# A mixture-of-experts stage on one core: TensorE branches on each expert's token count

## The chip, the cores and the metric

The kernel runs on one core of one Trainium2 chip. The metric is the device time of one execution in microseconds, given as the median of several runs. The profile is of one execution, taken by the hardware profiler; its span runs from the first to the last instruction and is a little shorter than the device time of the same execution.

The engines are TensorE (PE; its weight loads are listed apart, as PEld), VectorE (DVE), ScalarE (ACT), GpSimd (POOL) and SyncE (SP). Each works through its own queue of instructions in order. A matmul loads a 128x128 stationary operand and streams the columns of the other operand through it. A float32 matmul stands in the trace as two passes, each a weight load and a MATMUL record; a transpose by the identity is one pass.

## What is computed

One layer: graph attention over 3327 nodes, then a mixture of 16 experts of which each token takes two. The second half is what the change touches:

```python
logits = jnp.einsum('bsd,de->bse', x, gate_w) + gate_b
probs = jax.nn.softmax(logits, axis=-1)
top_probs, top_idx = jax.lax.top_k(probs, 2)
top_probs = top_probs / jnp.sum(top_probs, axis=-1, keepdims=True)
dispatch = jnp.sum(jax.nn.one_hot(top_idx, n_experts) * top_probs[..., None], axis=-2)
h1 = jnp.einsum('bsd,edh->bseh', x, w1)
h2 = jnp.einsum('bsd,edh->bseh', x, w2)
hidden = jax.nn.silu(h1) * h2
expert_out = jnp.einsum('bseh,eho->bseo', hidden, w3)
return jnp.einsum('bseo,bse->bso', expert_out, dispatch)
```

A token has 256 features, the hidden size is 512, all in float32. The inputs are fixed, and so is the routing. Evaluated on them, the reference sends these numbers of tokens to the experts 0 to 15:

```
351 473 404 471 511 387 336 393 505 414 372 404 387 375 473 398     (sum 6654 = 2 x 3327)
```

## The kernel before, in words

The first part (the graph attention and the routing, lines 153 to 447) ends with a table: `index[:, e, t]` holds, for expert `e` and row tile `t` of 128 places, the token that stands in each place, or a number out of bounds where the place is empty. An expert has 512 places (`CAP`), four row tiles (`CT`). `count` (L433) is the number of tokens of each expert. From it `chunks` and `more` say whether an expert has more than 512; for these inputs none has, and the second loop behind L533 is jumped over.

The second part works through the 16 experts, one after the other:

- `begin(e)` calls `fetch` (L465): four indirect DMAs on POOL (L468) gather the expert's rows, with their gate weights, into one of three buffers `xe0`, `xe1`, `xe2`, used in turn. Two short DVE instructions (L472 `hit`, L474 `weight`) then take the gate weight out of the rows; `hit` waits for all four DMAs.
- `turned` (L477): eight transposes on TensorE (L482) into PSUM, two ACT copies (L483), give `xte`, the transposed tokens, 2 blocks of 128 features by 512 places.
- `up` (L486): for each of four blocks `j` of 128 hidden units, four matmuls (L494; two blocks of features, for `w1` and for `w2`) give `p1` and `p2`, each 128x512 in PSUM. ACT makes `s = silu(p1)` (L497), DVE makes `hid[:, j] = s * p2` (L498). `p1` and `p2` have two PSUM buffers each.
- `down` (L501): for each of four row tiles `t`, four matmuls (L506; one for each `j`) give `py`, 128x256, in one of two PSUM buffers. DVE scales it by the gate weight into `y` (L509), and POOL adds it to the rows of `out` by an indirect DMA (L510); places that are out of bounds are not written.
- `load_expert` (L144): three DMAs on SP bring the next expert's weights.

The program gives a scheduler the instructions; it decides the order in each engine's queue and puts the semaphore waits. In the built program before the change the order on TensorE is, for every expert, up(e), the transposes for e+1, down(e), without any other work between them. On DVE `hit` for a later expert stands among the instructions of down, and on POOL the four gathers for a later expert stand next to the four additions to `out`.

All 512 places are multiplied, empty or not: the empty rows of `xe` hold zeros or old, finite data, and their results are not written.

## Time and profile before

| | |
|---|---|
| median of 3 runs | 642.27 us (642.19 to 642.32) |
| the profiled execution | 642.2 us; its span 640.4 us |
| first transpose of the expert stage (L482) | 279.0 us after the start of the span |
| last matmul of the expert stage (L506) | ends at 631.0 us |
| mean granted TensorE clock | 0.959 |

A line of a group gives the source line, the engine and the operation, the tile written and the tiles read, the shape and the count; behind the bar the busy time in us and the mean duration of one in ns; behind the second bar the time that the engine stood idle just before such instructions, and what ended most of it. MATMUL records overlap, so their mean is longer than their distance. An engine name with a q behind it (PEldq, SPq) means an instruction that the engine's sequencer does by itself, as a branch, a register load or a wait.

### The profile page before, as it was taken

To read this page: it belongs to the slowest core of one execution; us is meant where nothing else is said; L and a number is where in the kernel's file an instruction comes from. 1 tells how busy PE (TensorE), PEld (TensorE's weight loads), DVE (VectorE), ACT (ScalarE), POOL (GpSimd) and SP (SyncE) were. 2 spreads that over 40 slices of the span, in tenths; PEclk is the share of its full clock that TensorE was granted. 3 is DMA by queue.
4 is the path that set the end of the run, shared out by engine and by line. 5 is a ranking of instruction groups with operands and counts; after the bars stand their busy time and mean duration, and the time that the engine had idled before them with its cause. 6 is when DMAs were issued, how large, how long until landed. Compare 5 with 4: busy or idle time off the path is not lost. (4 is left out here: it accounts for less than half of the span.)

```text
span 640.4 us, 8294 instructions
## 1 busy us (share of the span) xinstructions
PE 584.6 (91%) x2906; PEld 430.7 (67%) x2907; DVE 271.4 (42%) x896; ACT 165.7 (26%) x472; POOL 209.4 (33%) x181
## 2 busy tenths in 40 slices
PE   1999999999999994459999999999999999999994
PEld 0778999999999993324566556656665666566653
DVE  4853576869687777722221222122212222222221
ACT  2666435151524244111111211121112111111110
POOL 2442100101010102055563356335533653333123
PEclk9999999899999996559999999999999999999998
DMA  7975488596858531124463445344534553444022
GB/s 251 389 217 200 140 272 271 165 328 225 296 178 317 188 95 64 67 54 122 90 148 94 102 112 153 104 94 109 142 101 98 118 145 100 85 97 117 8 30 28
DMA packets 65006, 94.71 MB, mean 148 GB/s; under 512 B 6331, under 2 KB 35135, under 8 KB 64960
## 3 DMA queue, kind: packets, MB, share of 16 engines
q1 hardware_dynamic: 51552, 79.75, 37.4%
q0 software_dynamic: 12288, 13.76, 12.8%
q10 hardware_dynamic: 1120, 0.61, 0.3%
q8 instruction: 24, 0.39, 0.2%
q14 instruction: 22, 0.18, 0.1%
HBM read 82.01 MB, written 15.26 MB: 152 GB/s over the span
## 5 line engine op out<-in xcount | busy, mean ns | idle before, releaser
L414 PE MATMUL pa<-hi,mk 128*128 128x258 f32 x676 | 169.1, 289 | 0.0
L415 PE MATMUL pa<-lo,mk 128*128 128x256 f32 x676 | 167.4, 287 | 1.5 <-DVE lo L215 1.5
L415 PEld LDWEIGHTS pa<-lo,mk 128*128 128x128 f32 x676 | 128.6, 190 | 1.9 <-DVE lo L215 1.7
L414 PEld LDWEIGHTS pa<-hi,mk 128*128 128x128 f32 x676 | 129.1, 191 | 0.2
L510 POOL DMA_INDIRECT out<-y,index x64 | 100.7, 1574 | 72.0 <-DVE y L509 55.3
L494 PE MATMUL p<-xte,w1e 128*128 128x512 f32 x256 | 122.2, 600 | 0.5 <-ACT xte L483 0.5
L494 PE MATMUL p<-xte,w2e 128*128 128x512 f32 x256 | 120.9, 595 | 1.5 <-DVE hid L498 1.5
L506 PE MATMUL py<-w3e,hid 128*128 128x256 f32 x512 | 113.2, 379 | 0.0
L498 DVE TENSOR_TENSOR hid<-s,p 128x512 f32<-128x512 f32 x64 | 43.9, 687 | 161.5 <-PE p L494 121.5
L468 POOL DMA_INDIRECT xe<-normed,index x64 | 65.5, 1023 | 132.4 <-PE pt L482 104.1
L497 ACT ACTIVATE s<-p 128x512 f32<-128x512 f32 x64 | 38.2, 597 | 258.5 <-PE p L494 258.5
L506 PEld LDWEIGHTS py<-w3e,hid 128*128 128x128 f32 x512 | 96.2, 190 | 12.8 <-issue 0.5
L494 PEld LDWEIGHTS p<-xte,w2e 128*128 128x128 f32 x256 | 48.8, 191 | 63.9 <-issue 60.8
L494 PEld LDWEIGHTS p<-xte,w1e 128*128 128x128 f32 x256 | 49.1, 192 | 55.8 <-issue 53.6
L375 DVE TENSOR_SCALAR mk<-sg 128x2048 fp32r<-128x2048 f32 (+2 forms) x49 | 52.5, 1072 | 30.5 <-PE pa L415 27.8
L509 DVE TENSOR_SCALAR y<-py,weight 128x256 f32<-128x256 f32 x64 | 30.1, 483 | 58.6 <-PE py L506 58.6
L172 POOL TENSOR_TENSOR rs_x<-rs_x,neg_half 128x4 f32<-128x4 f32 (+1 forms) x14 | 16.2, 1154 | 78.5 <-DVE rs_x L171 61.9
L172 POOL TENSOR_TENSOR rs_hp<-rs_hp,neg_half 128x4 f32<-128x4 f32 (+1 forms) x7 | 6.8, 969 | 107.2 <-DVE pay L333 49.4
L213 PE MATMUL ph<-w_sb,xnt 128*128 128x260 f32 x104 | 28.2, 414 | 1.5 <-DVE er L216 1.2
L266 ACT ACTIVATE hp<-csum,c 128x64 f32<-128x64 f32 x104 | 25.7, 334 | 13.8 <-DVE c L262 13.8
L177 ACT ACTIVATE pay<-x,rs_x 128x256 f32<-128x256 f32 x26 | 13.7, 591 | 59.8 <-DVE rs_x L173 59.8
L483 ACT COPY xte<-pt 128x512 f32<-128x512 f32 x32 | 17.2, 589 | 38.1 <-PE pt L482 38.1
(123 smaller groups left out, 442.8 us busy)
## 6 DMA issues: line engine op xcount, KB each, us to landing
sg<-in_adj_t SPq DMA_DIRECT2D x36, 1024.0 KB, 6.4
w1e<-in_ffn_w SPq DMA_DIRECT2D x16, 512.0 KB, 3.4
w2e<-in_ffn_w SPq DMA_DIRECT2D x16, 512.0 KB, 4.2
w3e<-in_ffn_w SPq DMA_DIRECT2D x16, 512.0 KB, 4.4
sg<-in_adj_t SPq DMA_DIRECT2D x12, 512.0 KB, 3.7
normed<-pay SPq DMA_DIRECT2D x6, 520.0 KB, 3.3
x<-in_x SPq DMA_DIRECT2D x6, 512.0 KB, 9.3
out<-x SPq DMA_DIRECT2D x6, 512.0 KB, 4.4
```

The costliest lines, as they stand in the source:

```text
L213: nc.tensor.matmul(ph, xnt[:, k, :], w_sb[:, k, :], start=(k == 0), stop=(k == KC - 1))
L266: nc.scalar.mul(hp[:, t, h * DH:(h + 1) * DH], csum[:, h * DH:(h + 1) * DH], c[:, 1, t, h:h + 1])
L375: nc.vector.tensor_scalar(mk[:, :M, :T * P], sg[:, :M, :T * P], 0.0, None, op0=ALU.is_gt)
L414: nc.tensor.matmul(pa[t], lhs, HI[mg][:, m, :], start=first, stop=False)
L415: nc.tensor.matmul(pa[t][:, :D], lhs, LO[mg][:, m, :], start=False, stop=last)
L468: nc.gpsimd.indirect_dma_start(out=xe[:, t, :], out_offset=None, in_=normed, in_offset=at_rows(idx, t), bounds_check=NP - 1, oob_is_err=False)
L494: nc.tensor.matmul(p, wt[:, k, j * P:(j + 1) * P], xt[:, k, :], start=(k == 0), stop=(k == KC - 1))
L497: nc.scalar.activation(s, p1, AF.Silu)
L498: nc.vector.tensor_mul(hid[:, j, :], s, p2)
L506: nc.tensor.matmul(py, hid[:, j, t * P:(t + 1) * P], w[2][:, j, :], start=(j == 0), stop=(j == JC - 1))
L509: nc.vector.tensor_scalar(y, py, weight[:, t:t + 1], None, op0=ALU.mult)
L510: i = nc.gpsimd.indirect_dma_start(out=out, out_offset=at_rows(idx, t), in_=y, in_offset=None, bounds_check=NP - 1, oob_is_err=False, comp ...
```

## The change

TensorE no longer multiplies all 512 places. From `count` DVE makes a table `width`: for each expert a number 0 to 4, which says the smallest of 384, 416, 448, 480 and 512 that holds its count, and a number 0 or 1, which says whether the count is over 384. TensorE loads these numbers into registers (32 loads in all). In `up`, for every `j`, it takes one of five arms, each with the same four matmuls at another number of columns. In `down`, at the last row tile, it takes one of two arms: the four matmuls, or none. The other engines do the same work as before, on the full 512 columns. So that they find finite numbers there, the PSUM tiles are no longer taken from a pool in turn, but are six fixed tiles, which DVE sets to zero once.

```diff
+WIDTHS = [384, 416, 448, 480, 512]
...
+    width = const.tile([P, 2, NE], I32, name="width")
...
         nc.vector.tensor_copy(count, pl[:, :NE])
 
+        bounds = tiny.tile([P, len(WIDTHS) - 1], F32, name="bounds", bufs=1)
+        over = tiny.tile([P, NE, len(WIDTHS) - 1], F32, name="over", bufs=1)
+        widthf = tiny.tile([P, 2, NE], F32, name="widthf", bufs=1)
+        nc.gpsimd.iota(bounds, pattern=[[WIDTHS[1] - WIDTHS[0], len(WIDTHS) - 1]], base=WIDTHS[0], channel_multiplier=0,
+                       allow_small_or_imprecise_dtypes=True)
+        nc.vector.tensor_tensor(over, count[:, :, None].to_broadcast([P, NE, len(WIDTHS) - 1]),
+                                bounds[:, None, :].to_broadcast([P, NE, len(WIDTHS) - 1]), op=ALU.is_gt)
+        nc.vector.tensor_reduce(widthf[:, 0], over, AX.X, ALU.add)
+        nc.vector.tensor_scalar(widthf[:, 1], count, float(CAP - P), None, op0=ALU.is_gt)
+        nc.vector.tensor_copy(width, widthf)
...
-        ps_h = ffn.enter_context(tc.tile_pool(name="ps_h", bufs=2, space=bass.MemoryType.PSUM))
-        ps_y = ffn.enter_context(tc.tile_pool(name="ps_y", bufs=2, space=bass.MemoryType.PSUM))
+        sums = ffn.enter_context(tc.tile_pool(name="sums", bufs=1, space=bass.MemoryType.PSUM))
...
-        def up(w, xt):
+
+        P1, P2, PY = ([sums.tile([P, size], F32, name=f"{name}{i}") for i in range(2)]
+                      for name, size in (("p1", CAP), ("p2", CAP), ("py", D)))
+        for p in P1 + P2 + PY:
+            nc.vector.memset(p, 0.0)
+
+        def arms(choice, n):
+
+            if choice is None:
+                yield n - 1
+            else:
+                yield from tc.Switch({mybir.EngineType.PE: choice}, n)
+
+        def up(w, xt, choice=None):
             t1, t2, _ = w
             hid = hidden.tile([P, JC, CAP], F32, name="hid")
             for j in range(JC):
-                p1 = ps_h.tile([P, CAP], F32, name="p1")
-                p2 = ps_h.tile([P, CAP], F32, name="p2")
-                for p, wt in ((p1, t1), (p2, t2)):
-                    for k in range(KC):
-                        nc.tensor.matmul(p, wt[:, k, j * P:(j + 1) * P], xt[:, k, :],
-                                         start=(k == 0), stop=(k == KC - 1))
+                p1, p2 = P1[j % 2], P2[j % 2]
+                for case in arms(choice, len(WIDTHS)):
+                    cols = WIDTHS[case]
+                    for p, wt in ((p1, t1), (p2, t2)):
+                        for k in range(KC):
+                            nc.tensor.matmul(p[:, :cols], wt[:, k, j * P:(j + 1) * P], xt[:, k, :cols],
+                                             start=(k == 0), stop=(k == KC - 1))
                 s = gates.tile([P, CAP], F32, name="s")
...
-        def down(w, hid, idx, weight):
+        def down(w, hid, idx, weight, choice=None):
             done = []
             for t in range(CT):
-                py = ps_y.tile([P, D], F32, name="py")
-                for j in range(JC):
-                    nc.tensor.matmul(py, hid[:, j, t * P:(t + 1) * P], w[2][:, j, :],
-                                     start=(j == 0), stop=(j == JC - 1))
+                py = PY[t % 2]
+                for case in arms(choice if t == CT - 1 else None, 2):
+                    for j in range(JC if case else 0):
+                        nc.tensor.matmul(py, hid[:, j, t * P:(t + 1) * P], w[2][:, j, :],
+                                         start=(j == 0), stop=(j == JC - 1))
...
+        def choice(i, e, top):
+            return nc.tensor.value_load(width[0:1, i, e:e + 1], min_val=0, max_val=top)
+
...
         for e in range(NE):
-            hid = up(WE[e], xt)
+            hid = up(WE[e], xt, choice(0, e, len(WIDTHS) - 1))
...
-            down(WE[e], hid, *ready.pop(e)[1:])
+            down(WE[e], hid, *ready.pop(e)[1:], choice(1, e, 1))
```

The scheduler orders a program of many blocks otherwise than one long block. This is TensorE's queue from the middle of the program, written down from the built program (`py(t,j)` is one matmul of row tile `t`; "waits" gives what a semaphore wait is for; e is an even expert, the pair repeats):

```
transposes for e+2 (last 4) around py(0,0) py(0,1) py(1,0) py(1,1) of e
switch up e+1, j=0
py(0,2) py(1,2) of e
switch up e+1, j=1
py(0,3) py(1,3) of e;  2 transposes for e+3;  py(2,0) of e: waits y of tile 0
switch tile 3 of e: waits y of tile 1
py(2,1) py(2,2) py(2,3) of e;  6 transposes for e+3
switch up e+1, j=2
py(0,0) py(1,0) of e+1
switch up e+1, j=3
py(0,1) py(1,1) of e+1
switch up e+2, j=0: its p2 waits hid of e+1, j=2
py(0,2) of e+1
switch up e+2, j=1: its p2 waits hid of e+1, j=3
py(0,3) py(1,2) py(1,3) of e+1;  py(2,0) of e+1: waits y of tile 0;  py(2,1)
switch tile 3 of e+1: waits y of tile 1
py(2,2) py(2,3) of e+1
switch up e+2, j=2;  4 transposes for e+4;  switch up e+2, j=3
```

And these are the queues of POOL and DVE over the same stretch:

```
POOL: gather 0 for the buffer that the transposes for e+2 left; add y2, y3 of e-1; gathers 1 2 3;
      add y0, y1 of e; gather 0 for the next buffer; add y2, y3 of e; gathers 1 2 3; add y0, y1 of e+1; ...
DVE:  hid of e j=2, j=3;  hit (waits the four gathers);  y0 y1 of e;  y2 y3 of e;  hid of e+1 j=0, j=1;
      hit (waits the next four gathers);  hid of e+1 j=2, j=3;  y0 y1 of e+1; ...
```

At the start the order is another one: before the first `up` stand five register loads, the transposes of expert 0 and two transposes of expert 1; then up of expert 0 for j=0 and j=1; then the other six transposes of expert 1, all eight of expert 2, and nine register loads among and behind them; then j=2 and j=3 of expert 0 with four matmuls of its down, and eight register loads; then up of expert 1.

## The prediction

> **What bounds the kernel now.** I read the page's engine line first, then the table of stretches from the middle of the expert stage, then the costliest groups, then the timelines of the queues that the change reorders.

> ```profile
> span 640.4 us, 8294 instructions
> PE 584.6 (91%) x2906; PEld 430.7 (67%) x2907; DVE 271.4 (42%) x896; ACT 165.7 (26%) x472; POOL 209.4 (33%) x181
> ...
> 320.00:400.00 80.00, 80.00 (x275) 49.34 (x274) 18.44 (x39) 12.65 (x22) 40.87 (x32) 1.00 0.50 121
> ...
> L494 PE MATMUL p<-xte,w2e 128*128 128x512 f32 x256 | 120.9, 595 | 1.5 <-DVE hid L498 1.5
> ...
> L506 PE MATMUL py<-w3e,hid 128*128 128x256 f32 x512 | 113.2, 379 | 0.0
> ```

> From 320 to 400 us TensorE is busy 80.00 of 80 us at clock 1.00, and its idle time before `py` is 0.0: the array is the whole cost there. An expert takes (631.0 - 279.0) / 16 = 22 us on average. The timeline gives 0.429 us from one 512-column pass to the next, 0.838 ns a column, and half that for a 256-column pass. Per expert: 32 passes x 0.429 + 32 x 0.2147 + 8 transposes x 0.11 = 13.7 + 6.9 + 0.9 = 21.5 us.

> ```profile
> L510 POOL DMA_INDIRECT out<-y,index x64 | 100.7, 1574 | 72.0 <-DVE y L509 55.3
> ...
> 326.45 1.00 POOL L468 DMA_INDIRECT xe<-normed,index  x1 [0.30 <-issue]
> 327.75 0.99 POOL L468 DMA_INDIRECT xe<-normed,index  x1 [0.30 <-issue]
> 329.05 1.62 POOL L510 DMA_INDIRECT out<-y,index  x1 [0.31 <-issue]
> 330.98 1.57 POOL L510 DMA_INDIRECT out<-y,index  x1 [0.31 <-DVE y L509]
> ...
> DVE hit L472 <- DMA xe<-normed,index: 57.2, 16, 7.0
> ...
> 330.17 0.17 DVE L472 SCALAR_TENSOR_TENSOR hit<-xe 128x8 f32<-128x8 f32 x1 [2.42 <-DMA xe<-normed,index]
> ```

> POOL needs 1.30 us from one gather to the next and 1.87 for an addition. `hit` waits 57.2 us in all for gathers and starts 2.2 to 4.2 us (median 2.84) after the last gather's start. Before the change this is hidden: the work behind it on DVE is not yet due.

> **Gain.** By the counts the widths are 384, 480, 416, 480, 512, 416, 384, 416, 512, 416, 384, 416, 416, 384, 480, 416: 6912 columns where there were 8192. 1280 x 32 passes x 0.838 ns = 34.3 us. Four experts (0, 6, 10, 13) have at most 384 and skip a tile of 8 passes, 1.72 us: 6.9. Sum 41.2 us, if TensorE stays fed.

> **DVE before the stage.** The six zeroings stand on DVE, with one more small instruction (`full`, 0.27 us) than before, ahead of `index`, on which the first gather waits. The 128x64 memset of before took 0.112 us, the 128x4 one 0.062: 0.83 ns an element gives 0.49 for 512 columns and 0.27 for 256, 2.5 in all; PSUM operations of those shapes took 0.687 and 0.483, together 3.7; lower end 2.1, if each starts 0.07 before the one ahead of it ends, as DVE's neighbours do here. I take 2.7 with `full`, bare on the path to the first gather. Three small ones of the width table stand there too, in the places of three of the `chunks` table, two of which move behind `index`.

> **Start.** Two transposes of expert 1 now stand before the first `up`, so it waits for a gather issued at 282.69: + 2.84 + 0.2 + a switch (0.83, below) = 286.5, where it was 283.38.

> ```profile
> 282.69 1.00 POOL L468 DMA_INDIRECT xe<-normed,index  x1 [0.30 <-issue]
> ...
> 287.81 0.21 PEld L494 LDWEIGHTS p<-xte,w2e 128*128 128x128 f32 x1 [0.52 <-issue]
> ...
> 290.50 1.00 POOL L468 DMA_INDIRECT xe<-normed,index  x1 [0.30 <-issue]
> ...
> L532 PEldq TENSOR_LOAD <-more x1: 493/493/493, 628.2 to 628.2; - x1
> L532 SPq FUSED_REGOPS  x1: 191/191/191, 275.9 to 275.9; - x1
> ...
> L533 PEldq COMPARE_BRANCH  x1: 373/373/373, 628.8 to 628.8; - x1
> L533 SPq COMPARE_BRANCH  x1: 50/50/50, 589.3 to 589.3; - x1
> ```

> Weight loads were 0.85 us apart until 287.8 and 0.43 after: for its first 4.4 us the array ran at half speed. So j=0 and j=1 (16 x 0.322 = 5.15, and 2.25 for the half speed) end at 293.9. Expert 2's transposes wait for the gather of 290.50, landed at 293.3; among and behind them stand register loads of 0.493 + 0.191 + 0.028 (assertion) = 0.71 us each: with seven of them and a switch j=2 starts at 299.2, the array idle for 3.8; eight more loads idle it for about 2. Expert 1 then begins at 308.1, where it was 308.8. But eight `py` matmuls are still owed (3.4), eight transposes already done (-0.9), and expert 0's whole saving of 5.15 is spent: -0.7 + 3.4 - 0.9 + 5.15 = 7.0. The idle may bring the half speed back: 0 to 2.3, I take 1.2. Start: 8.2. The other nine loads run ahead under queued matmuls; uncovered they would be 6.4.

> **The new DVE waits.** In the new order `hit` for a later expert stands on in-order DVE ahead of work that TensorE needs.
> - A: ahead of y0, y1 of experts 4, 6, 8 and 10. From the transposes that free the buffer: POOL 0.30, gather 1.30, two additions 3.74, two gathers 2.60 to the last one's start, 2.84 landing, `hit` 0.17, y0 0.48: 11.4. TensorE has 8 `py` and 3 transposes (3.77) and two up blocks of 8 x 416 x 0.838 ns = 2.79: 9.35. Wait 2.1, with handoffs 2.3; four: 9.1.
> - B: ahead of `hid` j=2 of experts 2, 3, 5, 7 and 9, for which the p2 of two switches later waits. From y0: four additions 7.48, three gathers 3.90, 2.84, `hit` 0.17, `hid` 0.69, handoffs 0.7: 15.8. TensorE has 4.6 of fixed work, 1.72 if the tile is kept, two up blocks of that expert and half of one of the next. For expert 5: 15.8 - 4.6 - 1.72 - 5.58 - 1.29 = 2.6; the five: 2.3, 1.4, 2.6, 3.9, 2.6 = 12.8.

> Together 22, and by the spread of the landing 18 to 27. Jumps on POOL between blocks lengthen both chains: 23 at about 0.1 (between SP's 0.05 and its 0.19 to the next instruction): 2.3.

> **The switches.** The trace has one compare and branch on TensorE's sequencer, 0.373 us; on SP it took 0.050. With register work a switch has 0.83 before its first matmul, 1.3 to the end. Where the sequencer is ahead of the array, as in the middle of `up` (it was 2.5 to 5.4 us ahead in the trace), that is hidden. It is not hidden at the switch of tile 3, behind the wait for y0, with 0.43 of `py` queued: 0.8 for each of eight even experts with y0's own handoff, 0.35 for each of eight odd, 0.5 for each of four empty arms: 11. Bounds: 4 by SP's row, 20 if each of 80 also shows 0.12 more.

> [...]

> **Sum**: -41.2 + 2.7 + 8.2 + 22 + 2.3 + 11 = +5. The profiled execution took 642.2 (span 640.4 and 1.8 around it), the median is 642.27: **647 us**. Its own range, adding the terms' bounds in part: 638 to 660.

> **Rivals.**
> - *Code misses (slower, far).* Each taken jump may find its target not yet loaded. The page counts instruction packets, 24 of 16 KB:

> ```profile
> q8 instruction: 24, 0.39, 0.2%
> ```

>   After the change TensorE's program has some 470 instructions an expert, arms not taken included: 29 packets of 256. The only jump of before, at 628.8, was followed by nothing for 2.3 us; that gap also holds the array's drain, so 2.3 is an upper end. At half of it, 29 x 1.15 = 33: 680 us; at 80 misses of 1.0 it passes 720. For it: that gap. Against: jumps that stay within a packet, and the sequencer's lead. It decides when a miss is longer than the lead. [...]
> - *The waits A and B do not come (faster).* If the last gather landed some 2.5 us earlier than my chains have it, both vanish: 647 - 22 - 2.3 = 623; if half of them, 635. For it: `hit` is never late in the trace of before, and POOL is busy for 33% only. Against: the spacing of 1.30 and 1.87 is the same in every expert, and a shorter `up` makes the cover shorter, not the chain.
> - *The narrower pass is no shorter.* If a pass were bound by its weight load, 34.3 us of the gain would be gone: 681. Against: weight loads took 0.19 us, a pass of 384 takes 0.322.

> **How the numbers follow.** Likeliest case 0.55, misses 0.18, no or half waits 0.23, no shorter pass 0.04. From 633 (half of the waits, some exposure less) to 680 (misses at half price) leaves out about 2 in 10. A measurement of this kernel tells a change of 0.2%, 1.3 us, from none: within it (641.0 to 643.6) I put 0.07, nearly all from the likeliest case; faster gets the second rival and a tenth of the likeliest, 0.29; slower the rest, 0.64.

> **What would show it.** The first gather 2.7 us later than 275.9. `up` passes 0.32 to 0.43 us apart by width; 0.43 everywhere speaks for the third rival. TensorE idle before `py` for y, and before `p2` for `hid`, about 2 us each at nine places, with `hit` just ahead of them on DVE; none of it: the second. An idle array around j=2 of expert 0 with register loads on PEldq. Branch records on PEldq of 0.3 to 0.5 us; gaps of over 1 us behind them with no wait, and many more than 24 instruction packets: the first. I am wrong if TensorE's idle time lies at places where no wait and no switch stands, or if the up blocks are paced by ACT or DVE, which still work on 512 columns: per j 0.60 and 0.69 us against 2.57, so far from it.

## The result and the profile after

The changed kernel takes 1075.85 us (median of 4 runs, 1072.97 to 1081.21) beside 642.23 of the kernel before on the same chip: 1.677 times as long, 95% interval 1.670 to 1.684. The prediction said 647, between 633 and 680. The sign was right; the size was off by 429 us. Ratios here and below leave out executions over 1.5% above the fastest of their kernel, which are four of the ten of `blocks`, its profiled one (650.4 us) among them.

The page of the profile after, the lines that answer to those shown of before (the rows of tenths are the span in 40 slices; PEclk is the granted TensorE clock):

```profile
span 1075.5 us, 9119 instructions
PE 705.3 (66%) x2874; PEld 474.7 (44%) x2875; DVE 269.6 (25%) x906; ACT 166.2 (15%) x472; POOL 210.0 (20%) x182
PE   3999999994455356566656664776666465675554
PEclk9999999996587667878888787786778768766777
q8 instruction: 297, 4.87, 2.5%
L521 PE MATMUL p<-xte,w1e 128*128 128x416 f32 (+3 forms) x256 | 182.5, 861 | 209.5 <-issue 207.2
L534 PE MATMUL py<-w3e,hid 128*128 128x256 f32 x480 | 141.9, 435 | 95.6 <-issue 95.0
```

Three things are to be seen. TensorE, which before stood idle 2.0 us before `up` and 0.0 before `down`, stands idle 207 us before the passes of `up` and 95 us before those of `down`, and what ended these waits is "issue": no DMA and no other engine that the profile shows, which leaves its own sequencer. The granted clock is at 0.5 to 0.8 from the tenth slice on, where the array is busy for 3 to 7 tenths of a slice. And the instruction queue (q8) moved 297 packets of 16 KB where it moved 24.

The view of the line under which the jumps are recorded (count, then least, median and greatest duration in ns, first and last start), for TensorE's sequencer and for DVE's:

```profile
L617 PEldq COMPARE_BRANCH  x160: 295/4497/5877, 289.1 to 1060.6; - x160
L617 PEldq FUSED_REGOPS  x80: 32/32/41, 289.0 to 1057.0; - x80
L617 DVEq COMPARE_BRANCH  x80: 41/41/53, 285.7 to 1057.2; - x80
```

There are two jumps to a switch, into the arm and out of it, 160 in all, with a median of 4.5 us. The 80 jumps of DVE, which only lead on to the next block, took 0.04 each. In a window from the middle, 600 to 660 us, the sequencer is hardly ever out of a jump, 14 of 4.5 us in 60 us:

```profile
L617 PEldq COMPARE_BRANCH  x14: 1507/4489/5209, 596.4 to 656.2; - x14
```

and the array beside it (start, duration, engine, line, operation, count of records, in brackets the idle time ahead):

```profile
614.00 2.92 PE L521 MATMUL p<-xte,w1e 128*128 128x384 f32 x4 [2.28 <-issue]
616.70 2.77 PE L521 MATMUL p<-xte,w2e 128*128 128x384 f32 x4
619.39 0.70 PE L495 MATMUL pt<-ident,xe 128*128 128x128 f32 x4
622.50 2.48 PE L521 MATMUL p<-xte,w1e 128*128 128x384 f32 x4 [2.40 <-issue]
...
655.83 2.93 PE L534 MATMUL py<-w3e,hid 128*128 128x256 f32 x6 [6.54 <-issue]
```

Adding up the 160 records gives 666 us; from the start of the first to the end of the last are 774 us. Which packets began to arrive during each jump, and where the jump led, I counted from the trace's records (which arm is taken follows from the counts):

| jump | number | packets begun in it | median us |
|---|---|---|---|
| into arm 384, the first behind the dispatch | 16 | 1 (two jumps: 0) | 2.9 (0.3) |
| into a later arm of `up` | 48 | 2 (four jumps: 1) | 4.5 |
| out of arm 512, the last before the common end | 8 | 1 | 3.1 |
| out of an earlier arm of `up` | 56 | 2 (one jump: 1) | 4.7 |
| tile 3, into and out of the arm with matmuls | 24 | 1 | 3.4 |
| tile 3, into the empty arm, and out of it | 4 + 4 | 0 (one jump: 1), then 2 | 1.7, then 4.7 |

A jump during which no packet began took 0.3 to 2.0 us (5 of them), with one 3.3 in the median (52), with two 4.6 (103). An arm is only some 18 instructions, while in the trace of before one packet began with every 254 instruction records of TensorE on average (5592 records from the first packet to the 23rd). Here 258 of the 297 packets began during the 160 jumps. How far apart the arms lie was not shown; what distance costs was tested (run 5).

### The profile page after: what moved, and what is told of

It is laid out like the page before. It is cut to its first block, busy times and chain, and to the rows that moved or that the text cites. A ratio compares the mean times of both kernels' runs of the same rounds, so it can differ in the third digit from the quotient of the medians.

```text
span 1075.5 us, 9119 instructions
## 1 busy us (share of the span) xinstructions
PE 705.3 (66%) x2874; PEld 474.7 (44%) x2875; DVE 269.6 (25%) x906; ACT 166.2 (15%) x472; POOL 210.0 (20%) x182
## 5 line engine op out<-in xcount | busy, mean ns | idle before, releaser
L521 PE MATMUL p<-xte,w1e 128*128 128x416 f32 (+3 forms) x256 | 182.5, 861 | 209.5 <-issue 207.2
L534 PE MATMUL py<-w3e,hid 128*128 128x256 f32 x480 | 141.9, 435 | 95.6 <-issue 95.0
L521 PEld LDWEIGHTS p<-xte,w1e 128*128 128x128 f32 x256 | 66.2, 285 | 276.3 <-issue 272.3
L521 PE MATMUL p<-xte,w2e 128*128 128x416 f32 (+3 forms) x256 | 144.3, 702 | 0.0
L521 PEld LDWEIGHTS p<-xte,w2e 128*128 128x128 f32 x256 | 72.5, 283 | 80.6 <-issue 78.7
L485 DVE SCALAR_TENSOR_TENSOR hit<-xe 128x8 f32<-128x8 f32 x16 | 2.7, 167 | 136.8 <-DMA xe<-normed,index 136.8
L495 PE MATMUL pt<-ident,xe 128*128 128x128 f32 x128 | 25.4, 318 | 11.7 <-DMA xe<-normed,index 8.9
L495 PEld LDWEIGHTS pt<-ident,xe 128*128 128x128 f32 x128 | 18.7, 165 | 25.2 <-issue 15.3
```

The source lines that it names most:

```text
L495: nc.tensor.transpose(pt[:, t * P:(t + 1) * P], xe[:, t, k * P:(k + 1) * P], ident)
L521: nc.tensor.matmul(p[:, :cols], wt[:, k, j * P:(j + 1) * P], xt[:, k, :cols], start=(k == 0), stop=(k == KC - 1))
L534: nc.tensor.matmul(py, hid[:, j, t * P:(t + 1) * P], w[2][:, j, :], start=(j == 0), stop=(j == JC - 1))
```

## Experiments

**Theory F:** TensorE's sequencer pays at the jumps during which instruction packets begin, 3.3 us in the median with one packet and 4.6 with two, and it pays for the packets; next to nothing else of the 434 us comes from the change. The jumps of a `Switch`, and those over code put in between (run 5), are called far below, a compare and branch with its arms close behind it near. Against it stand the order and its waits, narrower passes that are no shorter, and jumps that are slow by their kind, near or far. Each run below computes the full result. The time of before was 642.4 to 642.8 beside each.

**1. Widths without a branch (`static`).**

```diff
-                yield from tc.Switch({mybir.EngineType.PE: choice}, n)
+                yield choice        # a constant: from the list of the counts
```

> Widths and the skipped tile as constants in the program, taken from the known counts; no register load and no branch on TensorE, one block; the width table, the zeroings and the six fixed PSUM tiles stay. Theory F (TensorE's taken jumps cost the fetch of 16 KB code packets, and next to nothing else of the change costs): 642.3 - 41.2 + 2.7 = 604, between 602 and 612, instruction packets near the 24 of before. Rival N (narrower passes are no shorter): only the four skipped tiles show, about 638. Rival P (the fixed PSUM tiles or the zeroings cost much): above 620, with TensorE waiting for ACT or DVE.

607.6 us (ratio 0.946, 0.943 to 0.949), 23 packets. The narrower passes are shorter: the gain is there. Of the 41.2 us, 34.8 arrive. The first gather started at 278.44 where it was 275.89 (2.6), and in expert 0 TensorE waited twice for `hid`, 1.46 and 2.58 us, where before it waited once, 1.53: 41.2 - 2.6 - 2.5 = 36.1. The other 1.3 are not explained. Rivals N and P fall.

**2. The same in 80 blocks (`blocks`).**

```diff
-                yield choice
+                with tc.block():
+                    yield choice
```

> As the run static, but each of the 80 places stands in a block of its own, so that the scheduler's order is nearly that of the changed kernel, without its jumps and register loads. By the prediction's terms for the new order (22 for the waits A and B, 2.3 for POOL, about 3 for the start without the loads): 604 + 27 = 631, between 622 and 640, with TensorE idle before py and p2 and hit just ahead on DVE. If these waits were an error of the prediction too: 604 to 612. Both fit theory F; it says how much of the 434 us the order has at most.

The ratio is 1.005 (1.001 to 1.009), which is 645.8 us; its ten runs lay between 640.8 and 653.7, with a median of 649.6. So the order costs about 38 us over `static`, more than the 27 expected, but a tenth of what was lost. Its waits are of the prediction's kind B; none of kind A, for `y`, shows here. DVE's and TensorE's timelines of the run, and its waits view:

```profile
449.17 0.17 DVE L486 SCALAR_TENSOR_TENSOR hit<-xe 128x8 f32<-128x8 f32 x1 [9.90 <-DMA xe<-normed,index]
449.27 1.28 DVE L527 TENSOR_TENSOR hid<-s,p 128x512 f32<-128x512 f32 x2
...
450.02 3.14 PE L523 MATMUL p<-xte,w2e 128*128 128x416 f32 x4 [3.74 <-DVE hid L527]
...
DVE hit L486 <- DMA xe<-normed,index: 121.9, 16, 11.9
```

`hit` stands at the head of DVE's queue for 9.90 us until the gathers land, the two `hid` behind it run late, and p2 waits 3.74 us for them. The four passes behind the wait take 3.14 us where 1.56 is usual for 416 columns. Before, `hit` waited 57.2 us in all and nothing was late. Run 7 has the same waits.

**3 and 4. The last tile alone, by computed jump (`t3_switch`) and by compare and branch (`t3_if`).** Both leave `up` at 512 columns. The second has

```diff
-                yield from tc.Switch({mybir.EngineType.PE: choice}, n)
+                with tc.If(choice > 0):
+                    yield 1
```

> Only the last row tile is dispatched (16 switches, 32 jumps); up stays at 512 columns. Theory F: dispatch and exit measured 3.4 + 3.4 us where the arm with matmuls is taken (12 experts) and 1.7 + 4.7 where the empty one is (4): 107 us of TensorE's sequencer, of which a lead of 2 to 5 us at each switch hides 32 to 80; with the 6.9 of skipped tiles and some 10 for order: 675 to 720. By the price of the prediction (0.5 to 0.8 us a switch): 645 to 655. About 32 to 48 instruction packets more than before.

> The same 16 decisions as in t3_switch by compare and branch, with the two arms close behind it in the code. Theory F: the targets lie in code already loaded, a branch costs about the 0.37 us of the trace of before: 640 to 652, hardly more packets than before (24 to 32). Rival B (any taken branch of TensorE costs some 4.5 us, near or far): 16 to 20 taken jumps, about as t3_switch less its second jump, 665 to 700.

718.9 us (1.119, 1.116 to 1.122) with 69 packets, against 655.5 us (1.019, 1.016 to 1.022) with 24. The jumps of the first run, then of the second:

```profile
L617 PEldq COMPARE_BRANCH  x32: 296/3490/4378, 306.5 to 700.1; - x32
```

```profile
L510 PEldq COMPARE_BRANCH  x28: 65/169/304, 308.0 to 641.2; - x28
```

The same 16 decisions on the same engine take 99.4 us of sequencer time in the one form and 4.1 in the other. In the second form a comparison that falls through takes 0.07 and a taken jump 0.17 to 0.30. 655.5 is above the 640 to 652 expected: TensorE waits for y in experts 7, 8, 9 and 11, 2.5 to 2.9 us each, and for `hid` at the start (1.7), by the new order. Rival B falls.

**5. The same compare and branch, with code in between (`t3_far`).** Runs 3 and 4 differ in the kind of the jump and in the packets moved, 69 and 24. This one keeps the kind of run 4 and changes the distance; it adds one comparison in the four experts whose tile is skipped:

```diff
-                with tc.If(choice > 0):
+                with tc.If(choice > 0) as cmp:
                     yield 1
+                with cmp.Else():
+                    with tc.If(choice > 1):     # never so
+                        for _ in range(25):
+                            yield 1
```

> As t3_if, with 100 matmuls that are never reached (400 instructions, 25 KB of code) in the arm that the exit jumps over: the same kind of branch, the same decisions, only the target is farther. Theory F (distance beyond the loaded code is what costs): the 12 exits over the dead code and the 4 jumps past it take 3 to 4.6 us each, with a packet or two fetched during them, and the lead hides a part: 675 to 700. Rival C (it is the computed jump of a Switch, its register arithmetic or its arms' alignment alone, that is slow, and a compare and branch is fast at any distance): as t3_if, 655 within 3, branches of 0.07 to 0.3 us.

682.3 us (1.064, 1.060 to 1.067), 49 packets: 27 us more than `t3_if`, for code that never runs. The comparison ahead of the tile, the exit over the dead code, and the jump past it are in these rows:

```profile
L510 PEldq COMPARE_BRANCH  x28: 65/230/4797, 306.0 to 670.9; - x28
L513 PEldq COMPARE_BRANCH  x4: 319/3560/3719, 306.3 to 620.1; - x4
```

The dead code is 400 instructions, by the 254 to a packet of 16 KB in the trace of before some 25 KB. Of the 16 jumps over it, ten took 3.4 to 4.8 us (each with one packet begun in it), one 2.3, and five 0.3 with none begun. So the kind of the jump is not what costs (rival C falls); nor is it a count of instructions skipped, since the same 400 cost 0.3 us in five places. What goes with the price is whether a packet begins during the jump.

**6. A hint ahead of the jump (`t3_hint`).** As `t3_switch`, with an order by hand (see 8) and

```diff
                 hid = up(WE[e], xt)
+                early = tc.switch_hint({mybir.EngineType.PE: pick}, 2)
...
-                yield from tc.Switch({mybir.EngineType.PE: choice}, n)
+                yield from tc.Switch({mybir.EngineType.PE: choice}, n, early)
```

> As t3_switch (16 computed jumps, up at 512), with the prefetch hint for each jump issued ahead of 12 matmuls of down instead of none, and the hand-written order. Theory F: a hint that comes early enough lets the code be there: the dispatch falls from 3.5 us to about 0.3, the exit, whose hint stands 0.1 us ahead of it, stays at 3.4 and is hidden in part by the lead: 640 to 690. Rival (the price is in the jump, not in the fetch): dispatch unchanged at 3.5, 700 to 720.

677.2 us (1.051, 1.044 to 1.057). The jumps, in and out, are in this row:

```profile
L627 PEldq COMPARE_BRANCH  x32: 308/1932/4585, 306.1 to 663.9; - x32
```

15 of the 16 jumps into an arm took 0.31 to 0.36 us with no packet begun in them. Four of these lead into the empty arm, where `t3_switch` took 0.3 already; the other eleven took 3.5 to 4.4 there. The 16th took 3.6 again. The jumps out took 1.9 to 2.5 in eleven experts, 4.0 to 4.6 behind the empty arms and in one more. The page counts 68 instruction packets, about as many as the 69 of `t3_switch`: the packets still come, but outside these jumps. The same eleven computed jumps cost 0.31 to 0.36 us with no packet begun in them and 3.5 to 4.4 without the hint, so here too the price goes with the packets. The time itself mixes the hint with the order.

**7. The whole change by compare and branch (`iftree`).**

```diff
+        def among(choice, a, b):
+            if b - a == 1:
+                yield a
+                return
+            m = (a + b) // 2
+            with tc.If(choice < m) as cmp:
+                yield from among(choice, a, m)
+            with cmp.Else():
+                yield from among(choice, m, b)
```

> The whole change, with all 80 decisions as compare and branch (a tree of two or three comparisons for the five widths) in place of the computed jumps; the scheduler's order as it falls. Theory F (the cost is code that a far jump has to fetch; near targets cost 0.07 to 0.30 us, as t3_if measured): as the run blocks, 649.6, with 23 register loads at the start on top, 5 to 15: 650 to 668, and under 60 instruction packets. Rival B (many branches add up, or a tree of five arms reaches over the loaded code): above 750, with over 100 packets.

656.0 us (1.021, 1.019 to 1.023), 43 packets. 232 branches take 41 us of sequencer time in all; one of them took 3.2 us, the others under 0.42. The jumps' form, and with it the packets, 297 against 43, is worth 1075.9 - 656.0 = 420 of the 434 us. With the jumps near, the waits of the new order show, and TensorE's timeline and waits have both kinds:

```profile
507.61 3.72 PE L548 MATMUL py<-w3e,hid 128*128 128x256 f32 x16 [1.45 <-DVE y L551]
525.28 2.93 PE L535 MATMUL p<-xte,w2e 128*128 128x384 f32 x4 [4.70 <-DVE hid L539]
...
PE p L535 <- DVE hid L539: 20.2, 6, 4.7
PE py L548 <- DVE y L551: 6.8, 4, 1.9
```

**8. The same with the order by hand (`iftree_m`), and the computed jumps with that order (`switch_m`).**

```diff
+        with tc.manual_schedule():
...
+                if e + 2 < NE:
+                    rows(XE[(e + 2) % 3], index[:, e + 2, :])      # the four gathers
+                picks = choice(0, e, len(WIDTHS) - 1), choice(1, e, 1)
+                hid = up(WE[e], xt, picks[0])
...
+                    ready[e + 2] = gate(XE[(e + 2) % 3], index[:, e + 2, :], float(e + 2))   # hit, weight
+                xt = turned(ready[e + 1][0])
+                down(WE[e], hid, *ready.pop(e)[1:], picks[1])
```

> As iftree, and the order of the expert stage written out by hand on every engine: per expert the gathers for e+2, two register loads, up, hit behind the last hid, the transposes for e+1, down. Theory F with the order as the second cost: the run static (607.6) plus up to 15 for branches and loads that show: 608 to 623, no wait for hid or y of over 1 us in the middle. If the order is not what cost blocks its 42 us over static: 645 to 665, as iftree.

> The changed kernel with its computed jumps, and the hand-written order of iftree_m. Theory F: the 160 jumps sum to 660 us of TensorE's sequencer in the changed kernel, more than the array's work, so the order can gain little: 1000 to 1090. Rival: the order and its waits are a large part of the 434 us: below 900.

615.9 us (0.959, 0.957 to 0.961) and 1098.5 us (1.710, 1.707 to 1.714). With near jumps the order is worth 40 us and the change pays; with far ones it is worth nothing, since the sequencer sets the pace (665.4 us of jumps, 295 packets). `switch_m` lies above its expected 1000 to 1090, and why it is 23 us slower than the changed kernel I did not follow up.

What is left in `iftree_m`, in TensorE's timeline from 300 us on, is all of one kind; these are its only idle stretches of over 1 us:

```profile
306.26 3.50 PE L540 MATMUL p<-xte,w1e 128*128 128x480 f32 x4 [2.49 <-issue]
427.45 1.64 PE L540 MATMUL p<-xte,w1e 128*128 128x416 f32 x4 [2.13 <-issue]
505.76 1.64 PE L540 MATMUL p<-xte,w1e 128*128 128x416 f32 x4 [2.14 <-issue]
562.66 3.37 PE L540 MATMUL p<-xte,w1e 128*128 128x480 f32 x4 [2.38 <-issue]
```

They follow experts 0, 6, 10 and 13, whose last tile is skipped: in the empty arm TensorE's sequencer has a semaphore instruction, whose record starts as the array's last matmul ends (303.8 and 303.77 us at the first, 560.3 and 560.28 at the last), the array then stands idle for 2.1 to 2.5 us, and in two of the four cases the next two matmuls, of 480 columns, take 3.4 to 3.5 us where 1.77 is usual. The row of these instructions, on the line of the empty arm:

```profile
L515 PEldq EVENT_SEMAPHORE  x4: 51/51/51, 303.8 to 560.3; - x4
```

Each skip saves 1.72 us and loses more. What the semaphore counts the profile doesn't name.

**9. Without the skip (`up_m`).** `iftree_m`, with the last tile always computed.

> As iftree_m, but the last row tile is always computed; only the widths are dispatched. In iftree_m the array's only idle stretches of over 1 us in the middle were the four empty arms, 2.1 to 2.5 us each (9.1), with slower passes behind them; they skip 6.9 us of work. 615.9 - 9.1 + 6.9 = 614, less up to 3 for the slower passes: 610 to 614. If the empty arms were not what these stretches wait for: 623.

608.0 us (0.947, 0.945 to 0.949): 34.8 us faster than before and 7.9 faster than with the skip, 2 below the range expected. With the skip go its 16 register loads and its comparisons too, which this run doesn't tell apart from the empty arms. In the middle TensorE is busy without a gap again (its windows: the stretch, then PE's busy time, PEld, DVE, ACT, POOL, the clock, the DMA share, GB/s):

```profile
320.00:400.00 80.00, 80.00 (x289) 51.87 (x288) 19.69 (x40) 13.85 (x24) 41.71 (x32) 1.00 0.54 125
400.00:480.00 80.00, 80.00 (x301) 54.12 (x300) 20.17 (x42) 13.85 (x24) 42.67 (x33) 1.00 0.53 130
```

In 80 us there are 289 and 301 matmul records where before there were 275. It chooses the widths at run time and is level with `static`, which has them as constants and skips the tile too. A version with twelve widths in steps of 16 (`up_m12`) needs more memory for its small tables than was left, 8.31 KB a partition beside 7.91, and has no time; what the jumps of a larger tree cost stays open.

## Why the prediction was wrong

- *What bounds the kernel, the gain.* Right. 41.2 us were to be had from the array; `static` shows 34.8 and where most of the rest went.
- *DVE before the stage.* 2.7 was taken; the first gather started 3.2 us later in the changed kernel, 2.6 in `static`. Counted from the end of POOL's last work before it, the gap was 12.71 us before and 14.63 in both, so 1.9 of it lies where the zeroings stand; the rest of the shift arose earlier.
- *The start and the new DVE waits.* 8.2 + 22 + 2.3 = 32.5 were taken. `blocks`, which has no register loads, lost about 38 to the order, and `iftree` 40 against `iftree_m`. The mechanism was right: in `iftree` TensorE waits for `y` at four places (6.8 us, 9.1 were forecast) and for `hid` at the five of kind B (20.1 us, 12.8 were forecast), in the experts that the prediction named. What it left out, but for 1.2 us at the start, is that passes behind a gap were slow here: four of 384 columns took 2.93 us in `iftree` behind a wait of 4.70, where 1.45 is usual in `iftree_m`. From 280 us to the end of the stage TensorE's busy time is 327.3 us in `iftree` and 311.5 in `iftree_m`, for the same matmuls, at a granted clock of 0.94 and 0.98; that makes 16 of the 40 us. The register loads were 0.68 us apart beside the 0.71 taken. In the changed kernel itself none of this shows, because the jumps are longer than the waits.
- *The switches: the step that failed.* The prediction took 0.83 us before the first matmul and 1.3 for a whole switch, from one branch record of 0.373 us, hid most of it under the sequencer's lead of 2.5 to 5.4 us, and counted 11 us, at most 20. Measured are two jumps of 4.5 us in the median to a switch, 666 / 80 = 8.3 us on average. The array has some 3.8 us of work for it at full clock ((16 x 21.5 - 41.2) / 80), so the lead is used up: TensorE stands idle 101 times with "issue" as the end of the wait, 302 us in all, and the sequencer is the bound. The record of 0.373 was a jump with no packet begun in it (0.17 to 0.30 where `t3_if` takes one); it said nothing of a jump during which packets begin.
- *The rival "code misses".* It named the place of the cost, with 0.18, and mis-sized it. It took the program's code as fetched once, 29 packets of 256 instructions (254 in the trace of before) at 1.15 us; in the changed kernel one or two packets begin during 155 of the 160 jumps, and the whole program moves 273 more than before. With its own upper price, 2.3 us, and one packet at each of 160 jumps it would have said 368 us more. The line "at 80 misses of 1.0 it passes 720" still counted one jump to a switch. The far jumps took 2.9 to 4.7 us in the median by kind, but for the way into the empty arm, the near ones of `t3_if` 0.07 us where they fall through and 0.17 to 0.30 where they are taken.
- *The sum of all other terms.* With the jumps near, the same change took 656.0 us, inside the likeliest case's own range of 638 to 660. It lies 48.4 us above `static`; 8.2 + 22 + 2.3 + 11 = 43.5 were taken for the start, the waits and the switches.

## What to carry to other kernels

Before a branch is put on an engine that sets the pace, ask where its target lies (400 instructions that never run, put in between, took `t3_if` from 655.5 to 682.3 us) and count every taken jump, the way out as well as the way in. See, too, whether the instruction packets in the page rise with the jumps: here they went from 24 to 297 with 160 computed jumps, and to 43 with the same choices by compare and branch. Close arms behind a compare and branch cost 0.07 to 0.3 us a jump in `t3_if`, and 64 choices by them left `up_m` at 608.0 us beside 607.6 without a branch; the computed jump of a Switch cost 2.9 to 4.7 us each way here in the median, but for the way into an empty arm. And look at what the division into blocks does to the other engines' order: by hand it gave back 40 us, as much as the change could gain.

## What the runs showed beside this

- A hint issued 12 matmuls ahead made the computed jump into an arm with matmuls cost 0.31 us at eleven of twelve; behind the hint that stands 0.1 us ahead of it, the jump out still took 1.9 to 4.6.
- Skipping work can cost more than the work: an empty arm with a semaphore instruction in it idled the array for 2.1 to 2.5 us to save 1.72.
- The array is slower too: in the changed kernel passes of 384 columns were 0.64 us apart around 615 us, where they are 0.32 in `static`, and from 280 to 1064 us the granted clock was 0.76, in `static` 0.98 over its stage. How much of the time this added was not measured.
